# Attention's output added in halves from two buffers, its last block by single chunks, ending six tiles from the end

## The chip, the cores and the metric

One Trainium2 chip, one of its cores. The time is device microseconds of one execution. A profiled execution gives, besides its time, the span from the first to the last recorded instruction, in which all positions below are told. The engines are TensorE (PE, with its weight loads PEld), VectorE (DVE), ScalarE (ACT), GpSimd (POOL) and SyncE (SP), which only issues DMAs.

## What is computed

The input x is 8 sequences of 1024 tokens with 256 numbers each, in float32. It is normalised by token, and the output is the sum of three things: x itself, a causal linear attention over each sequence (16 heads of 16, kernel elu + 1), and a mixture of 8 experts of which each token takes 2.

```python
xn = _layernorm(x)
# attention
q = jax.nn.elu(q) + 1.0
k = jax.nn.elu(k) + 1.0
kv_cumsum = jnp.cumsum(jnp.einsum('blhd,blhe->blhde', k, v), axis=1)
out = jnp.einsum('blhd,blhde->blhe', q, kv_cumsum) / denom[..., None]
out.reshape(Bx, Lx, HIDDEN) @ Wo.T
# experts: c holds two weights a token
h = jax.nn.silu(gate) * up
out = jnp.einsum('bse,besh->bsh', c, jnp.einsum('besi,eih->besh', h, W2))
x = x + attention(xn) + experts(xn)
```

## The kernel before

**Attention** goes by blocks of 512 tokens (NBLK = 16, two to a sequence), each of four chunks of 128. `block_steps` (L1033) cuts a block into 9 steps: four project q, k and v and spread the denominators (`rden`, eight DMAs on SP's queue), one computes the first chunk's scores and closes the block before, four weigh the chunks. With one step after the last block there are LAST = 145 steps. `attend` (L1009) ends a chunk: two matmuls with Wo into `a_ps` (L1016), and ScalarE copies the result into a quarter of the tile `at` (L1021). `at` is a tile of four chunks, from a pool with one buffer. After the fourth chunk GpSimd issues one DMA of 512 KB that adds `at` to the rows of the output (L1027); of the last block three chunks go first (384 KB) and the fourth by itself (128 KB, L1025). A chunk is closed one step after it is weighed, the fourth in the fifth step of the next block.

**The experts** (FFN) go by tiles of 128 rows sorted by expert: NM = 132 tiles, 25 of the first four blocks and then 107. For tile j, `ffn_step` (L1345) issues the gathers of rows (`xg`) and of their weights and moments (`entry`) some tiles ahead on GpSimd's queue (L1217, L1222), the two 512 KB weight matrices of tile j + 2 on SP's queue (L1288, five buffers), and between them the DMA transpose of the normalised rows (L1249). TensorE makes `gu_ps` from them (L1307), ScalarE and VectorE make hT = silu(gate) * up (L1315, L1318), TensorE makes `y_ps` of the tile before (L1326), VectorE multiplies it by the routing weight into `y` (L1333, five buffers), and GpSimd adds those rows to the output by an indirect DMA (L1337, `ffn_store`). For the first 25 tiles and the first attention blocks the sums go to an accumulator in memory, `acc_d`, which is copied to the output after tile 26 (L1440); all others go to the output `out_dram`.

**Order.** The loop over tiles (L1389) calls `attend_upto(n)` ahead of each tile's `ffn_step`: it makes attention steps until n are made, at most one a tile except at the steps that may go together. From tile READ = 22 on, n rises in a straight line from 23 to 144 at tile 130, and the rest falls to tile 131 (L1433). Apart from the first stage, a scheduler places the instructions on the engines in an order near that of the program, and it inserts the waits. Every DMA that adds to `out_dram` waits until the one before it that touched `out_dram` has landed, whatever rows it writes; and an instruction that waits on GpSimd's queue holds back all that stand behind it there: stores, gathers, entries. The last tile is cut in two on TensorE, with the y matmuls of tile 130 between its two halves (`last`, L1296).

Of the kernel before, what the change touches and what calls it, by code (L numbers as in the profile page):

```python
# [46 lines left out]
F32 = mybir.dt.float32  # L47
# [4 lines left out]
ALU = mybir.AluOpType  # L52
AX = mybir.AxisListType

P = 128
# [9 lines left out]
def tile_attention_moe(  # L65
# [14 lines left out]
    nc = tc.nc  # L80
    B, L, H = x.shape
# [4 lines left out]
    NCH = TB // P  # L86
    N = B * L
    NBLK = N // TB
# [10 lines left out]
    NM = NF - NR  # L99
# [11 lines left out]
    one = ctx.enter_context(tc.tile_pool(name="one", bufs=1))  # L111
# [31 lines left out]
    for t in range(FB):  # L143
        xbs[t] = e_one.tile([P, NCH, H], F32, name=f"xb{t}")
        step = NCH // 2 if t == 0 else NCH
        for c in range(0, NCH, step):
            some = slice(c, c + step)
            in_order(nc.sync.dma_start(out=xbs[t][:, some, :], in_=xf[t][:, some, :]))

    def load_x(t, queue):  # L150
        xbs[t] = f_x.tile([P, NCH, H], F32, tag="xb", name=f"xb{t}")
        in_order(queue.dma_start(out=xbs[t], in_=xf[t]))
# [15 lines left out]
    for t in range(FB, FB + 2):  # L168
# [8 lines left out]
        out=causal, in_=causal, pattern=[[1, P]], compare_op=ALU.is_ge,  # L177
# [5 lines left out]
        out=before, in_=before, pattern=[[1, P]], compare_op=ALU.is_ge,  # L183
# [8 lines left out]
        out=own, in_=own, pattern=[[-HD, HALF]], compare_op=ALU.is_ge,  # L192
# [3 lines left out]
        out=own, in_=own, pattern=[[HD, HALF]], compare_op=ALU.is_ge,  # L196
# [105 lines left out]
    def moments(t, n):  # L302


        def small(name, *shape, dtype=F32):
            return f_two.tile([P, n * NCH, *shape], dtype, tag=name, name=name)

        less, rstd = (tab[:, t * NCH : (t + n) * NCH, w] for w in (1, 2))
        st = small("st", 6)
        mv = small("mv", 2)  # L310
        for c in range(n * NCH):
            nc.vector.bn_stats(st[:, c, :], xbs[t + c // NCH][:, c % NCH, :])
            nc.vector.bn_aggr(mv[:, c, :], st[:, c, :])
        v = small("v")
        nc.vector.tensor_scalar(v, mv[:, :, 1], EPS_NORM, None, ALU.add)
        half = small("half")
        nc.vector.tensor_scalar(half, v, -0.5, None, ALU.mult)
        bits = small("bits", dtype=I32)
        nc.vector.tensor_scalar(bits, v.bitcast(I32), 1, None, ALU.arith_shift_right)
        nc.vector.tensor_scalar(bits, bits, -1.0, float(0x5F3759DF), ALU.mult, ALU.add)  # L320
        y = bits.bitcast(F32)
        for i in range(4):
            sq = small("sq")
            nc.vector.tensor_tensor(sq, y, y, ALU.mult)
            nc.vector.tensor_tensor(sq, sq, half, ALU.mult)
            y_new = small(f"y{i % 2}") if i < 3 else rstd
            nc.vector.scalar_tensor_tensor(y_new, sq, 1.5, y, ALU.add, ALU.mult)
            y = y_new
        yield
        nc.vector.scalar_tensor_tensor(less, mv[:, :, 0], -1.0, rstd, ALU.mult, ALU.mult)  # L330
        yield

    def normalise(t):
        xb = xbs.pop(t)
        less, rstd = (tab[:, t * NCH : (t + 1) * NCH, w] for w in (1, 2))
        for c in range(NCH):
            if t < FB and (c % 2 == 0 or t == FB - 1):
                nc.vector.tensor_scalar(
                    xb[:, c, :], xb[:, c, :], rstd[:, c : c + 1], less[:, c : c + 1],
                    ALU.mult, ALU.add,  # L340
                )
            else:
                nc.scalar.activation(
                    xb[:, c, :], xb[:, c, :], AF.Identity, bias=less[:, c : c + 1],
                    scale=rstd[:, c : c + 1],
                )
        scaled[t] = xb
# [47 lines left out]
    def logits_turned(t):  # L395
        lgT = f_two.tile([P, P], F32, tag="lgT", name="lgT")
        nc.scalar.copy(lgT, logits(t))
        tp = ps_y.tile([P, P], F32, tag="y", name="lg_t")
        nc.tensor.transpose(tp, lgT, ident)
        return tp  # L400
# [398 lines left out]
    blocks = {}  # L799
# [207 lines left out]
    ats = {}  # L1007

    def attend(t, c, oT):  # L1009


        if c == 0:
            ats[t] = one.tile([P, NCH, H], F32, tag="at", name=f"at{t}")
        a_ps = ps_y.tile([P, H], F32, tag="y", name="a_ps")
        for hh in range(2):
            nc.tensor.matmul(  # L1016
                a_ps, lhsT=oT[:, hh, :], rhs=wo_sb[:, hh, :],
                start=(hh == 0), stop=(hh == 1),
            )
        at = ats[t]  # L1020
        nc.scalar.copy(at[:, c, :], a_ps)  # L1021
        to = acc_f if t < FB and not copied else of
        if t == NBLK - 1 and c >= NCH - 2:
            some = slice(0 if c == NCH - 2 else c, c + 1)
            nc.gpsimd.dma_start(out=to[t][:, some, :], in_=at[:, some, :], accum_op=ALU.add)  # L1025
        elif c == NCH - 1:
            nc.gpsimd.dma_start(out=to[t], in_=at, accum_op=ALU.add)  # L1027
        if c == NCH - 1:
            del ats[t], blocks[t]

    behind = []

# [28 lines left out]
    LAST = NBLK * STEPS + 1  # L1061
# [11 lines left out]
    def attend_upto(n, apart=True):  # L1073
        first = True
        while steps_made[0] < min(n, LAST):
            if apart and not first and steps_made[0] % STEPS not in TOGETHER:
                break
            next(steps)
            steps_made[0] += 1
            first = False  # L1080
# [90 lines left out]
    for a in range(4):  # L1171
        some = slice(a * E // 4, (a + 1) * E // 4)
        in_order(
            nc.sync.dma_start(
                out=w2_sb.rearrange("p (c h) -> p c h", h=H)[
                    :, a * E * IC // 4 : (a + 1) * E * IC // 4, :
                ],
                in_=w2[some].rearrange("e (c p) h -> p (e c) h", p=P),
# [7 lines left out]
    def copy_rows(a, b):  # L1186
# [6 lines left out]
        out=tab_d[0].rearrange("(p j i) w -> p j (i w)", j=2, i=FT),  # L1193
        in_=tab.rearrange("p (j i) w -> p j (i w)", j=2)[:, :, 0 : FT * 3],
# [33 lines left out]
    def ffn_norm(j):  # L1228
        in_order(
            nc.scalar.activation(  # L1230
                xg[j], xg[j], AF.Identity, bias=entry[j][:, 1:2], scale=entry[j][:, 2:3]
            )
        )
# [3 lines left out]
    def ffn_halves(j):  # L1237

        halves[j] = ffn2.tile([P, 2, H], U16, tag="half", name="half")
        nc.vector.tensor_copy(  # L1240
            halves[j], xg.pop(j).bitcast(U16).rearrange("p (h b) -> p b h", b=2)
        )
# [143 lines left out]
    LISTS = NBLK - FB  # L1386
    READ = LISTS + 10
    AHEAD = 2 + LISTS // 2 + 3 * (READ - LISTS) // 2
    for j in range(NM + 1):  # L1389
        if j + 1 < TURNED:  # L1390
            ffn_norm(j + 1)
        if TURNED <= j + 2 < NM:
            ffn_norm(j + 2)
            ffn_halves(j + 2)
        t = FB + j
        counting = FB < t <= NBLK and t % ROUND == 0
        if counting and t == NBLK:
            for _ in routing:
                pass
        if 0 < j and t < NBLK:  # L1400
            if j % 2 == 0:
                with tc.issue_after((last_token if j < 4 else last_masked)[0].ins):
                    for _ in moments(t, 2):
                        pass
            normalise(t)
            turn(t)
            if t + 5 < NBLK:
                load_x(t + 5, nc.scalar)
            add_logits(t, 1, logits_turned(t))
            if (t + 1) % ROUND == 0:  # L1410
                routing = route(t + 1 - ROUND, t + 1)
                next(routing)
        if j == LISTS:
            in_order(
                nc.sync.dma_start(
                    out=tab_d[1][1 : 1 + NS * P, :].rearrange("(p i) w -> p (i w)", p=P),
                    in_=tab.rearrange("p i w -> p (i w)"),
                )
            )
            in_order(nc.sync.dma_start(out=tab_d[1][0:1, :], in_=before[0:1, 0:3]))  # L1420
            lists = second_batch(taken)
        if LISTS <= j < READ:
            next(lists)
        if LISTS <= j < LISTS + NBLK - FB:
            t = FB + j - LISTS
            rows = slice(t * TB, (t + 1) * TB)
            in_order(nc.sync.dma_start(out=out_rows[rows, :], in_=x_rows[rows, :]))
        if j < LISTS:
            attend_upto(3 + j // 2)
        elif j < READ:  # L1430
            attend_upto(AHEAD - 3 * (READ - j - 1) // 2)
        else:
            attend_upto(AHEAD + (LAST - 1 - AHEAD) * (j - READ + 1) // (NM - 1 - READ) + j // (NM - 1))  # L1433
        ffn_step(j, LATE if N1 < j <= N1 + LATE else 0)
        if counting and j < LISTS:
            for _ in routing:
                pass
        if j == N1 + 1:
            copied.append(j)
            in_order(nc.sync.dma_start(out=out_rows[0 : FT * P, :], in_=acc_d[:, :]))  # L1440
# [54 lines left out]
```

## Time and profile before

| what | us |
|---|---|
| three timed runs, median (lowest to highest) | 1266.21 (1262.2 to 1268.4) |
| the profiled execution | 1262.54 |
| its span | 1260.7 |
| TensorE busy | 1217.8 (97%) |
| GpSimd busy | 522.2 (41%) |
| ScalarE waiting for the DMA of `at` before its copy L1021 | 27.7, in 6 places |

In the profile's lines a group is named by line, engine and operation, with what it writes and reads (`out_dram<-at` is the DMA that adds attention's output, `out_dram<-y,dst_i` a store of a tile's rows). The page's second part cuts the span into 40 slices with a digit for the busy tenths of each; its fourth part follows the work that ended last back to its releasers. A timeline line gives the start, the duration, the engine, and in brackets how long the engine had been idle before and what ended that. DMAs issued by GpSimd run on after their instruction has ended, so the instruction's own duration (1.6 us for a store) is not the transfer's.

Of the page's list of DMA issues, these bear on the change: `out_dram<-at` thirteen times with 512 KB, once with 384 KB and once with 128 KB; `acc_d<-at` twice with 512 KB; `out_dram<-y,dst_i` 107 times; `w<-in_w_dram` 264 times with 512 KB.

### The profile page before, as it was taken

The page shows a single profiled execution, that of the slowest core. Times are in us where ns is not written, and L with a number is a line of the kernel's source. Part 1 is how long each engine was busy: PE and PEld are TensorE (multiplying, and loading weights), DVE is VectorE, ACT ScalarE, POOL GpSimd, SP SyncE. Part 2 cuts the span into 40 slices and gives each one's busy share as a digit, 9 for nine tenths or more (in the row PEclk, how much of TensorE's full clock was granted, in tenths as well). Part 3 has the DMA queues.
Part 4 walks back from the last instruction along what each step waited for, and adds up shares of the span by engine and source line. Part 5 has one row for each costly group of instructions (what it writes and reads, how often), then busy time and mean ns, then how long its engine had stood idle before and what let it go on. Part 6 is the DMA issues. An engine that isn't in the chain of part 4 may idle for free.

```text
span 1260.7 us, 29753 instructions
## 1 busy us (share of the span) xinstructions
PE 1217.8 (97%) x11460; PEld 1058.2 (84%) x11460; DVE 674.5 (54%) x1541; ACT 560.9 (44%) x1068; POOL 522.2 (41%) x460
## 2 busy tenths in 40 slices
PE   7799999999999999999999999999999999999994
PEld 5578887787898989988888989989888889899884
DVE  7677589864354554545453545545453545445451
ACT  5666475461534526262624426262626344252620
POOL 4734233233334544443535444444443444443422
PEclk9899999999999999999999999999999999999998
DMA  9798565557788796979799797879896877969782
GB/s 334 278 288 255 174 192 118 181 157 224 212 191 196 173 235 155 228 176 219 161 196 207 164 224 155 219 180 207 184 215 161 197 193 168 218 157 231 166 177 35
DMA packets 203934, 245.84 MB, mean 195 GB/s; under 512 B 72946, under 2 KB 127858, under 8 KB 203506
## 3 DMA queue, kind: packets, MB, share of 16 engines
q1 hardware_dynamic: 161010, 191.79, 52.5%
q0 software_dynamic: 38032, 43.22, 24.2%
q10 hardware_dynamic: 4752, 8.91, 2.1%
q8 instruction: 94, 1.54, 0.5%
q14 instruction: 46, 0.38, 0.1%
HBM read 187.91 MB, written 44.29 MB: 184 GB/s over the span
## 4 chain that ended last, share of the span: by engine, by line
PE 87%; DVE 5%; ACT 3%; DMA 3%; issue 1%; POOL 0%; SPq 0%; POOLq 0%; DVEq 0%; ACTq 0%
PE gu_ps L1307 37%; PE y_ps L1326 17%; PE s_ps L937 5%; PE o_ps L974 5%; PE a_ps L1016 5%; PE zq L820 4%; PE zkv L836 4%; PE zkk L836 4%; PE o_ps L956 2%; DMA xb<-in_x_dram 1%; PE tp L358 1%; DMA out_dram<-y,dst_i 1%; PE tp L883 1%; PE lg_ps L378 1%; DMA out_dram<-at 1%
## 5 line engine op out<-in xcount | busy, mean ns | idle before, releaser
L1307 PE MATMUL gu_ps<-xgT,w 128*128 128x128 f32 x4224 | 509.3, 277 | 0.5 <-ACT xgT L1270 0.5
L1307 PEld LDWEIGHTS gu_ps<-xgT,w 128*128 128x128 f32 x4224 | 489.1, 192 | 20.0 <-issue 14.4
L1337 POOL DMA_INDIRECT out_dram<-y,dst_i x107 | 175.2, 1638 | 328.3 <-DVE s_sb L944 103.3
L1326 PE MATMUL y_ps<-w_sb,hT 128*128 x1056 | 251.0, 380 | 1.8 <-DVE hT L1318 1.6
L1217 POOL DMA_INDIRECT xg<-in_x_dram,src_i x132 | 129.1, 978 | 240.1 <-DVE half L1240 109.9
L1326 PEld LDWEIGHTS y_ps<-w_sb,hT 128*128 128x128 f32 x1056 | 190.4, 191 | 23.6 <-DVE hT L1318 2.0
L944 DVE TENSOR_TENSOR s_sb<-s_ps,causal 128x512 f32<-128x512 f32 x256 | 159.8, 682 | 81.5 <-PE s_ps L937 75.2
L1315 ACT ACTIVATE hT<-gu_ps 128x512 f32<-128x512 f32 x132 | 78.8, 597 | 277.1 <-PE gu_ps L1307 207.5
L1222 POOL DMA_INDIRECT entry<-tab_d,of_i x107 | 106.4, 995 | 42.3 <-issue 31.4
L1318 DVE TENSOR_TENSOR hT<-gu_ps,hT 128x512 f32<-128x512 f32 x132 | 90.3, 684 | 61.9 <-PE gu_ps L1307 33.0
L1240 DVE COPY half<-xg 128x512 uint16<-128x512 uint16 x105 | 47.5, 453 | 134.9 <-ACT xg L1230 134.9
L1333 DVE TENSOR_SCALAR y<-y_ps,entry 128x256 f32<-128x256 f32 x132 | 63.6, 482 | 99.8 <-PE y_ps L1326 99.5
L1021 ACT COPY at<-a_ps 128x256 f32<-128x256 f32 x64 | 23.8, 372 | 172.1 <-PE a_ps L1016 123.7
L937 PE MATMUL s_ps<-qm,kT 32*128 32x256 f32 x1024 | 85.4, 404 | 0.5 <-DVE hT L1318 0.4
L1258 ACT COPY xgT<-halfT 128x512 uint16<-128x512 uint16 x105 | 79.7, 759 | 6.5 <-DMA halfT<-half 6.5
L1230 ACT ACTIVATE xg<-xg,entry 128x256 f32<-128x256 f32 x132 | 78.6, 596 | 4.1 <-DMA entry<-tab_d,num_i 3.4
L1016 PE MATMUL a_ps<-wo_sb,oT 128*128 128x256 f32 x256 | 68.2, 387 | 3.0 <-DVE oT L991 2.7
L974 PE MATMUL o_ps<-s_sb,va 128*32 128x128 f32 x2048 | 69.9, 276 | 0.0
L974 PEld LDWEIGHTS o_ps<-s_sb,va 128*32 128x32 f32 x2048 | 52.3, 109 | 17.9 <-issue 15.3
L937 PEld LDWEIGHTS s_ps<-qm,kT 32*128 32x128 f32 x1024 | 50.6, 184 | 18.6 <-issue 9.3
L1337 POOL DMA_INDIRECT acc_d<-y,src_i x25 | 40.9, 1637 | 53.0 <-DVE y L1333 15.1
L836 PE MATMUL zkv<-wkv_sb,xnT 128*128 128x256 f32 x256 | 59.6, 386 | 0.0
(228 smaller groups left out, 1353.9 us busy)
## 6 DMA issues: line engine op xcount, KB each, us to landing
w<-in_w_dram SPq DMA_DIRECT2D x264, 512.0 KB
rden<-over SPq DMA_DIRECT2D x128, 64.0 KB
xnT<-xnT_d SPq DMA_DIRECT2D x15, 512.0 KB
out_dram<-at POOLq DMA_DIRECT2D x13, 512.0 KB
out_dram<-in_x_dram SPq DMA_DIRECT2D x12, 512.0 KB
xnT_d<-xnT ACTq DMA_DIRECT2D x11, 512.0 KB
xb<-in_x_dram SPq DMA_DIRECT2D x9, 512.0 KB
w_sb<-in_w_dram SPq DMA_DIRECT2D x4, 1024.0 KB
```

The costliest lines, as they stand in the source:

```text
L836: nc.tensor.matmul(z[:, i, :], lhsT=xnTs[t][:, k, bass.ts(c + i, P)], rhs=wkv_sb[:, k, a, :], start=(k == 0), stop=(k == KC - 1),)
L937: nc.tensor.matmul(s_ps[r][:, hh].rearrange("p a l -> p (a l)"), lhsT=kT[rows, hh, span], rhs=qm[rows, hh, :, span], start=True, stop=True,)
L944: last_masked[0] = nc.vector.tensor_tensor(sm, s_ps[r].rearrange("p k a l -> p (k a) l"), causal_b, ALU.mult)
L974: nc.tensor.matmul(o_ps[32 * r : 32 * r + 32, hh, :], lhsT=va[:, c, 4 * hh + r, a, :], rhs=s_sb[r][:, 2 * hh + a, :], start=(first and a = ...
L1016: nc.tensor.matmul(a_ps, lhsT=oT[:, hh, :], rhs=wo_sb[:, hh, :], start=(hh == 0), stop=(hh == 1),)
L1217: rows = nc.gpsimd.indirect_dma_start(out=xg[j], out_offset=None, in_=x_rows[:, :], in_offset=bass.IndirectOffsetOnAxis(ap=src_i[:, i : i ...
L1222: nc.gpsimd.indirect_dma_start(out=entry[j], out_offset=None, in_=table[:, :], in_offset=bass.IndirectOffsetOnAxis(ap=num_i[:, i : i + 1], ...
L1258: nc.scalar.copy(xgT[j].bitcast(U16).rearrange("p k (l b) -> p b k l", b=2), halves.pop(j).rearrange("p (b k) l -> p b k l", b=2),)
L1307: done = nc.tensor.matmul(ps[:, i, :], lhsT=w13[:, k, bass.ts(i, P)], rhs=xgT[j][:, k, :], start=(k == 0), stop=(k == KC - 1),)
L1318: nc.vector.tensor_tensor(hT, gu[1], hT, ALU.mult)
L1326: done = nc.tensor.matmul(y_ps, lhsT=hT[:, i, :], rhs=w2_sb[:, bass.ds(e * (IC * H) + i * H, H)], start=(i == 0), stop=(i == IC - 1),)
L1337: nc.gpsimd.indirect_dma_start(out=rows[:, :], out_offset=bass.IndirectOffsetOnAxis(ap=dst_i[:, i : i + 1], axis=0), in_=ys.pop(j), in_off ...
```

## The change

`at` becomes two tiles of two chunks, `at0` and `at1`, each with a buffer of its own. After every second chunk the two are added by a DMA of 256 KB. Of the last block each chunk is added by itself (128 KB). The count of attention steps is taken from a new function, `spread(j)`: a straight line from tile 22 to 140 steps at tile 116 (SLOW = NM - 16), then one step in every two tiles, so that the last of 145 is made ahead of tile 125's `ffn_step`.

```diff
-        if c == 0:
-            ats[t] = one.tile([P, NCH, H], F32, tag="at", name=f"at{t}")
+        half = c // 2
+        if c % 2 == 0:
+            ats[t, half] = one.tile([P, NCH // 2, H], F32, tag=f"at{half}", name=f"at{half}")
...
-        at = ats[t]
-        nc.scalar.copy(at[:, c, :], a_ps)
+        at = ats[t, half]
+        nc.scalar.copy(at[:, c % 2, :], a_ps)
         to = acc_f if t < FB and not copied else of
-        if t == NBLK - 1 and c >= NCH - 2:
-            some = slice(0 if c == NCH - 2 else c, c + 1)
-            nc.gpsimd.dma_start(out=to[t][:, some, :], in_=at[:, some, :], accum_op=ALU.add)
-        elif c == NCH - 1:
-            nc.gpsimd.dma_start(out=to[t], in_=at, accum_op=ALU.add)
+        alone = t == NBLK - 1
+        if alone or c % 2:
+            some = slice(c, c + 1) if alone else slice(c - 1, c + 1)
+            nc.gpsimd.dma_start(
+                out=to[t][:, some, :], in_=at[:, some.start % 2 : c % 2 + 1, :],
+                accum_op=ALU.add,
+            )
...
+    SLOW = NM - 16
+
+    def spread(j):
+        most = LAST - 5
+        if j <= SLOW:
+            return AHEAD + (most - AHEAD) * (j - READ + 1) // (SLOW - READ + 1)
+        return min(LAST, most + (j - SLOW + 1) // 2)
+
...
-            attend_upto(AHEAD + (LAST - 1 - AHEAD) * (j - READ + 1) // (NM - 1 - READ) + j // (NM - 1))
+            attend_upto(spread(j))
```

More of the change, by code (lines that the diff above doesn't have):

```diff
@@ L1019, in attend @@
             )
-        at = ats[t]
-        nc.scalar.copy(at[:, c, :], a_ps)
+        at = ats[t, half]
+        nc.scalar.copy(at[:, c % 2, :], a_ps)
         to = acc_f if t < FB and not copied else of
-        if t == NBLK - 1 and c >= NCH - 2:
-            some = slice(0 if c == NCH - 2 else c, c + 1)
-            nc.gpsimd.dma_start(out=to[t][:, some, :], in_=at[:, some, :], accum_op=ALU.add)
-        elif c == NCH - 1:
-            nc.gpsimd.dma_start(out=to[t], in_=at, accum_op=ALU.add)
+        alone = t == NBLK - 1
[5 more added lines that the diff above has]
+            )
+        if c % 2:
+            del ats[t, half]
         if c == NCH - 1:
-            del ats[t], blocks[t]
+            del blocks[t]
     behind = []
```

## Prediction

> **What bounds the kernel now.** I read the slices of the span first, then busy time by stretch, then the chain that ended last, and then GpSimd's timeline, because the chain ends there.
>
> ```profile
> span 1260.7 us, 29753 instructions
> PE 1217.8 (97%) x11460; PEld 1058.2 (84%) x11460; DVE 674.5 (54%) x1541; ACT 560.9 (44%) x1068; POOL 522.2 (41%) x460
> ...
> PE   7799999999999999999999999999999999999994
> ```
>
> TensorE is idle at the two ends only. The stretches say it in figures (after the window: its length, then busy us of PE, PEld, DVE, ACT, POOL, the granted clock, the DMA share and GB/s):
>
> ```profile
> 400.00:1000.00 600.00, 600.00 (x5624) 532.70 (x5623) 290.14 (x534) 262.91 (x441) 271.52 (x224) 1.00 0.85 191
> 1000.00:1229.00 229.00, 229.00 (x2291) 203.04 (x2290) 113.72 (x211) 92.69 (x157) 90.71 (x74) 1.00 0.83 191
> 1229.00:1246.00 17.00, 15.80 (x131) 14.10 (x129) 5.14 (x11) 2.45 (x5) 5.48 (x4) 1.00 0.32 41
> 1246.00:1261.00 15.00, 0.00 (x0) 0.00 (x0) 0.17 (x1) 0.00 (x0) 3.15 (x2) 0.66 0.24 26
> ```
>
> From 400 to 1229 us TensorE has no idle time at a granted clock of 1.00; a wait removed from another engine there shortens nothing. The last 15 us hold no matmul at all. The chain that ended last shows what they hold (start us, us, what):
>
> ```profile
> 1234.06 5.74 DMA out_dram<-at
> ...
> 1240.55 3.95 DMA out_dram<-y,dst_i
> ...
> 1245.05 3.03 DMA out_dram<-at
> ...
> 1248.83 3.90 DMA out_dram<-y,dst_i
> ...
> 1253.78 1.25 POOL out_dram L1337
> ```
>
> Every addition to the output, a tile's rows (y) or attention's block (at), waits until the one before has landed. The last y matmul begins at 1243.66 and lasts 1.99, so TensorE ends at **T = 1245.65**, and 15.05 us follow. Two attention pieces of 384 and 128 KB stand among the last stores. GpSimd's timeline says where the queue came from:
>
> ```profile
> 1201.28 1.58 POOL L1337 DMA_INDIRECT out_dram<-y,dst_i  x1 [6.50 <-DVE y L1333]
> 1207.06 1.39 POOL L1027 DMA_DIRECT2D out_dram<-at  x1 [4.20 <-DMA out_dram<-y,dst_i]
> 1219.86 1.66 POOL L1337 DMA_INDIRECT out_dram<-y,dst_i  x1 [11.40 <-DVE s_sb L944]
> ```
>
> Block 14's 512 KB held the chain from 1207.06 to 1219.86, 12.8 us.
>
> **The change, part by part.**
>
> *Halves.* Blocks 0 to 14 make 30 pieces of 256 KB instead of 15 of 512 KB, and the last block four of 128 KB instead of two: 34 issues for 17. GpSimd spends 1.39 us on a 512 KB issue and 0.91 us on the last, 128 KB one, so 17 more cost it at most 24 us of 1260, in idle time (41% busy). Each piece waits on ACT's copy and on the landing before it; the gather and the stores behind it on GpSimd wait too. A gather is issued three to four tiles before its rows are normalised, some 30 us, and y has five buffers, so a piece of 5 to 7 us reaches nobody. If it did, ScalarE's normalisation and then TensorE would wait for rows.
>
> *Two buffers.* ScalarE's copy L1021 waits 27.7 us in 6 places for "DMA out_dram<-at". That goes. In those stretches TensorE is already busy all the time: worth nothing, bounded by 0 and 27.7, and I take 0 because TensorE shows no idle time to give back.
>
> *Denser attention.* Up to tile 116 attention makes 117 steps in 95 tiles (1.23 a tile) instead of 121 in 109 (1.11); then one step in two tiles; the last after tile 125's start. The matmuls are the same in number, and in the built order of the changed kernel a step still stands between gu and y groups. Changes between full and 32-wide matmuls cost about 0.1 us each and shift by a handful either way: 0, within 1 us. So TensorE's end stays at T if it is fed.
>
> *The end.* After store 121 can be issued, TensorE still has, by the chain's rows: the step with chunk 2 (a_ps 0.86, o_ps 0.54, 0.90, 0.24: 2.5), two FFN tiles (gu 3.57 and y 1.73: 5.30 each, 10.6), chunk 3's 0.86, six FFN tiles alone (31.8), and the halved last tile (1237.34 to 1245.65: 8.3). That is 54.0 us. With 0.48 for the multiplication by the weight and 0.3 to the issue, store 121 may go at T-53.2 and store 131 at T+0.85. In between the chain must carry ten stores (121 to 130) and two 128 KB pieces. From issue to next issue a quiet store takes **4.65** (1248.83 to 1253.48) and a quiet 128 KB piece **3.78** (1245.05 to 1248.83). After the last issue 7.2 us follow (1253.48 to 1260.70).
>
> - All quiet: the chain keeps up until the last three stores, which come at only 3.6 and 4.6 us spacing (T-7.5, T-3.8, T+0.85). Store 129 at T-7.5 plus two of 4.65 gives T+1.8 for store 131, the end T+9.0, against T+15.05: **6.0 us gained**.
> - Loaded: weights run until about T-12. GpSimd's timeline has stores that wait for each other under load:
>
> ```profile
> 1158.83 1.62 POOL L1337 DMA_INDIRECT out_dram<-y,dst_i  x1 [3.06 <-DVE s_sb L944]
> ...
> 1163.45 1.63 POOL L1337 DMA_INDIRECT out_dram<-y,dst_i  x1 [0.45 <-issue]
> ...
> 1168.09 1.62 POOL L1337 DMA_INDIRECT out_dram<-y,dst_i  x1 [0.46 <-DVE y L1333]
> ```
>
> 4.62 and 4.64, with an entry and a gather between them. Others take longer: 1201.28 to 1207.06 (5.78), 1117.75 to 1124.17 (6.42, behind a gather). So a loaded store is bounded by 4.62 and 6.42. I take **5.0**, nearer the quiet end, as no block of 512 KB and no spreading of denominators (rden) falls in this stretch, while weights come faster than before. A loaded 128 KB piece lies between 3.78 and half of the slowed 512 KB one (6.4); I take 4.2, near the row of its own size. Seven loaded stores (121 to 127), three quiet ones and two pieces: 35.0 + 13.95 + 8.4 = 57.35. Store 131 goes at T+4.15, the end is T+11.4 = 1257.05: **3.6 us gained**.
>
> One rule speaks against the change. The Trainium skill, "DMA: Bandwidth & Descriptors", section on the anatomy of one DMA on the GpSimd path, gives each DMA a fixed cost near 2 us plus its bytes at 436 GB/s, so that cutting transfers up multiplies the fixed part. The rows agree in kind: 128 KB took 3.03 us and 384 KB 5.74, a straight line that leaves 1.7 us at no bytes. By the page four pieces of 128 KB would take 9.2 us where 384 and 128 KB took 5.2, by the rows 12.1 where 8.8; both make the chain's work longer, and only where it lies can make it cheaper. By the page's 2.3 us a piece in place of 4.2 the sum would gain 6.0.
>
> **Sum.** The span falls from 1260.7 to 1257.1, the profiled execution from 1262.54 to 1258.9. The three timed runs have the median 1266.21, 3.7 above the profiled one; I take the same 3.6 off it: **1262.6**.
>
> **Rivals.**
>
> - *The chain stays quiet* (4.65 throughout): 6.0 gained, **1260.2**. For it: 4.62 and 4.64 above at a DMA share of about 0.7. Against it: FFN tiles alone ask for more. Chance 0.22.
> - *The chain is the bound and overflows.* Pairs of tiles with one step bring two stores and a piece in about 14.2 us (two tiles 10.6, a step 3.6). From 117 on the chain carries eleven loaded stores, three quiet and four pieces in 81.6 us; it ends as late as before at 5.3 us a store with 4.4 a piece (58.3 + 13.95 + 17.6 - 81.6 + 7.2 = 15.4 after T). At 5.8 and 4.5, the queue late enough that two more stores go quiet, nine loaded: 52.2 + 23.25 + 18.0 - 81.6 + 7.2 = 19.1 after T, 4 us **slower**, about **1270.3**; at 6.4 some 10 us. It decides from 5.3 us. For it: 5.78 and 6.42; against it: those had a gather or rden alongside. Chance 0.15.
> - *The weights come late.* An FFN tile alone needs 1.05 MB of weights, and 0.13 each of gather, store, its read and the transpose: 1.57 MB in 5.3 us is 296 GB/s. The stretches show 335 in the first 32 us, 299 at 1150, but 263 to 268 at 1206 to 1214. At 268 a tile takes 5.9 us, 0.6 more on six tiles: 3.6 us later, less what lies loaded ahead (two and a half tiles of buffers). I price it at 2.5, which leaves a gain of about 1: **1265**. Chance 0.12.
> - *The likeliest*, 3.6 gained: chance 0.51.
>
> **Numbers.** Predicted 1262.6. 0.5% is 6.3 us, about what a measurement of this kernel can tell from no change (its runs lie 6.2 us apart). The quiet case stands on that edge: 0.09 of its 0.22 lies beyond it, and 0.07 of the likeliest: faster 0.16. The overflowing chain passes 6.3 in the larger part of its chance, 0.09, with 0.01 from late weights: slower 0.10. Same 0.74. The range takes in the quiet case less 2 us of spread and the overflowing chain at 5.8: 1258 to 1270.5.
>
> **What would show it.** Right: TensorE without idle time from 400 us to its last matmul, its end within 1 us of 1245.65, the copies' wait for the DMA of at gone, no at among the last eight additions, 9 to 13 us after the last matmul. The quiet case shows GpSimd waiting for y (DVE) before the last stores but two; the overflow shows each of the last ten stores waiting for the one before, 5.5 us and more apart. Late weights would show TensorE idle before gu (a DMA of w as the releaser) in the last 40 us. I am wrong altogether if the middle changes: if rows arrive late behind the more numerous pieces, if the copy of the accumulator to the output at 337 us is held up by a piece that now goes to the accumulator, or if the denser attention stalls TensorE.

## The result and the profile after

The changed kernel takes 1274.23 us (median of 20 runs, 1266.43 to 1277.9) where the kernel before took 1264.95 beside it (20 runs, 1261.54 to 1274.27): a ratio of 1.0062, 95% interval 1.0049 to 1.0076. It is slower by 0.6%, where 3.6 us of gain were forecast. The profiled execution took 1275.46 us with a span of 1273.8, 13.1 more than the span before. That is more than the 9.3 us between the medians: the profiled execution of the kernel before lies 2.4 us under its median, that of the changed kernel 1.2 over its own.

The page and the stretches of the changed kernel, in the columns known from before:

```profile
span 1273.8 us, 29815 instructions
PE 1221.6 (96%) x11460; PEld 1063.4 (83%) x11460; DVE 674.6 (53%) x1541; ACT 560.0 (44%) x1068; POOL 545.9 (43%) x477
...
PE   7899999999999999999999999999999999999991
```

```profile
400.00:1229.00 829.00, 828.58 (x7943) 737.98 (x7942) 404.59 (x749) 352.99 (x597) 375.77 (x309) 1.00 0.86 190
1229.00:1246.00 17.00, 16.15 (x115) 15.02 (x113) 4.50 (x8) 3.10 (x5) 4.74 (x3) 1.00 0.53 104
1246.00:1274.00 28.00, 0.24 (x2) 0.00 (x0) 0.48 (x1) 0.00 (x0) 7.78 (x5) 0.55 0.22 24
```

TensorE is as full as before: 0.42 us idle in the 829 us from 400 to 1229, and its last matmul ends at 1246.24 (1245.65 before). Nearly all of the 13.1 us lies behind that: 27.5 us from the last matmul to the end, where there were 15.05. The last stretch holds five GpSimd instructions, and they are stores. GpSimd's timeline from the first late store on (start, duration, instruction, in brackets its idle time before and what ended it; gathers and entries between them are left out, here and in the timelines below):

```profile
1167.86 1.63 POOL L1342 DMA_INDIRECT out_dram<-y,dst_i  x1 [3.38 <-DVE s_sb L944]
...
1173.59 0.97 POOL L1027 DMA_DIRECT2D out_dram<-at  x1 [2.81 <-DMA out_dram<-y,dst_i]
...
1178.65 1.62 POOL L1342 DMA_INDIRECT out_dram<-y,dst_i  x1 [2.74 <-DVE y L1338]
...
1190.03 1.06 POOL L1027 DMA_DIRECT2D out_dram<-at  x1 [3.81 <-ACT hT L1320]
...
1196.69 1.62 POOL L1342 DMA_INDIRECT out_dram<-y,dst_i  x1 [4.25 <-DMA out_dram<-at]
...
1209.73 0.96 POOL L1027 DMA_DIRECT2D out_dram<-at  x1 [2.46 <-ACT xgT L1263]
...
1217.06 1.63 POOL L1342 DMA_INDIRECT out_dram<-y,dst_i  x1 [5.02 <-DMA out_dram<-at]
...
1227.28 0.97 POOL L1027 DMA_DIRECT2D out_dram<-at  x1 [1.59 <-issue]
1233.78 1.63 POOL L1342 DMA_INDIRECT out_dram<-y,dst_i  x1 [5.53 <-DVE y L1338]
1238.38 1.56 POOL L1342 DMA_INDIRECT out_dram<-y,dst_i  x1 [2.97 <-issue]
...
1261.83 1.56 POOL L1342 DMA_INDIRECT out_dram<-y,dst_i  x1 [2.96 <-issue]
1266.37 1.56 POOL L1342 DMA_INDIRECT out_dram<-y,dst_i  x1 [2.98 <-DMA out_dram<-y,dst_i]
```

The four single pieces of the last block are the lines with `at`. Their periods, from the piece's start to the next addition's, are 5.06, 6.66, 7.33 and 6.50: 6.39 in the mean. The seven stores from 1167.86 on (117 to 123) take 5.77 in the mean. The last weights are issued at 1230.47, and from 1236 to 1240 the DMA traffic has fallen to 34 GB/s. The seven stores 124 to 130, from 1233.78 on, take 4.66 in the mean (4.48 to 4.60, one of them 5.42): the same instruction, quiet. The last issue at 1266.37 leaves 7.43 to the end.

The clearest view is how late each store starts after VectorE has made its y (worked out from the two engines' timelines, us):

| store | 117 | 118 | 119 | 120 | 121 | 122 | 123 | 124 | 125 | 126 | 127 | 129 | 131 |
|---|---|---|---|---|---|---|---|---|---|---|---|---|---|
| before | 0.3 | 12.2 | 11.7 | 7.3 | 0.3 | 0.3 | 1.1 | 1.7 | 0.3 | 11.4 | 8.0 | 3.4 | 7.3 |
| after | 3.7 | 5.4 | 4.8 | 9.2 | 11.5 | 16.4 | 16.8 | 21.7 | 21.0 | 17.3 | 17.4 | 18.6 | 19.2 |

Before, a block of 512 KB throws the chain back by some 12 us, and three tiles later it is on time again. After, the pieces are smaller and the chain is never on time again. The reason is the distance between the tiles: y of tile 115 and y of tile 131 are 129.6 us apart before (8.1 a tile) and 96.4 after (6.03), because the attention steps that lay between those tiles have been made earlier. A store of 5.77 in a tile of 6.03 leaves 0.26 us for everything else.

The wait that the change was aimed at is gone. ScalarE's copies before and after, from the list of its waits (in total, times, longest):

```profile
ACT at L1021 <- DMA out_dram<-at: 27.7, 6, 5.5
```

```profile
ACT at L1022 <- PE a_ps L1017: 137.4, 52, 6.0
```

No line of the changed kernel has a copy wait for the DMA. No gain shows for it; TensorE had not been waiting for it.

### The profile page after: what moved, and what is told of

Same layout as the page of the kernel before. It is cut to its first block, busy times and chain, and to the rows that moved or that the text cites. A ratio compares the mean times of both kernels' runs of the same rounds, so it can differ in the third digit from the quotient of the medians.

```text
span 1273.8 us, 29815 instructions
## 1 busy us (share of the span) xinstructions
PE 1221.6 (96%) x11460; PEld 1063.4 (83%) x11460; DVE 674.6 (53%) x1541; ACT 560.0 (44%) x1068; POOL 545.9 (43%) x477
## 5 line engine op out<-in xcount | busy, mean ns | idle before, releaser
L1027 POOL DMA_DIRECT2D out_dram<-at x29 | 37.1, 1280 | 81.6 <-DMA out_dram<-y,dst_i 39.9
L974 PEld LDWEIGHTS o_ps<-s_sb,va 128*32 128x32 f32 x2048 | 52.8, 110 | 18.1 <-issue 15.5
```

The lines of the kernel that those rows point to most:

```text
L974: nc.tensor.matmul(o_ps[32 * r : 32 * r + 32, hh, :], lhsT=va[:, c, 4 * hh + r, a, :], rhs=s_sb[r][:, 2 * hh + a, :], start=(first and a = ...
```

## The experiments

The overflow of the chain was a rival in the prediction. What had to be told apart was why its transfers were so long, and which part of the change fills the chain. The first theory, L, is the load: weights for fast tiles take the DMA engines while the additions run. Its rival, Q, is GpSimd's own queue, the gathers and entries between the stores. The runs lay on four chips. On one the kernel before took 1265.16 us, on the others 1286.22, 1286.04 and 1285.09. So each ratio is against the kernel before on the same chip, and tails (from the last matmul's end to the end of the span) are compared within one chip first.

### Half of the change at a time

The halves and the single pieces, with the pace of before:

```diff
-            attend_upto(spread(j))
+            attend_upto(AHEAD + (LAST - 1 - AHEAD) * (j - READ + 1) // (NM - 1 - READ) + j // (NM - 1))
```

> The halves and two buffers, with the last block by single chunks, at the old pace (last attention step at tile 131). Theory L (load): an addition to the output takes 5.8 us for a store and 6.4 us for a 128 KB piece only while tiles without attention pull weights in fast; at the old pace of 8.3 us a tile the chain of additions keeps up, and 12 to 17 us follow TensorE's last matmul: 1262 to 1267 us, within 0.3% of the kernel before. Theory N (number): seventeen more additions make the chain too long wherever they stand: over 20 us after the last matmul, 1269 us or more.

Measured: 1286.28 us, ratio 0.998 (0.9951 to 1.0008), a tail of 16.2, as theory L has it.

The pace alone, with the kernel before's one tile `at`, blocks of 512 KB and the last block as 384 and 128 KB:

```diff
-            attend_upto(AHEAD + (LAST - 1 - AHEAD) * (j - READ + 1) // (NM - 1 - READ) + j // (NM - 1))
+            attend_upto(spread(j))
```

> The new pace alone (117 steps up to tile 116, then one in two tiles, the last at tile 125), with whole blocks of 512 KB in one buffer and the last block in 384 and 128 KB. Theory L: the pace makes the loss by itself: 20 us or more after the last matmul, 1269 to 1277 us. Theory N: with only two pieces among the last sixteen stores instead of four the chain fits: 9 to 14 us after the last matmul, 1259 to 1264 us.

Measured: 1289.08 us, ratio 1.0009 (0.9981 to 1.0037), a tail of 26.0. GpSimd's timeline of this run has the long tail with no single piece in it but the last:

```profile
1221.42 1.41 POOL L1025 DMA_DIRECT2D out_dram<-at  x1 [4.56 <-DMA out_dram<-y,dst_i]
1229.10 1.64 POOL L1337 DMA_INDIRECT out_dram<-y,dst_i  x1 [4.90 <-DVE y L1333]
1236.41 1.62 POOL L1337 DMA_INDIRECT out_dram<-y,dst_i  x1 [3.12 <-DMA out_dram<-y,dst_i]
1243.35 0.97 POOL L1025 DMA_DIRECT2D out_dram<-at  x1 [4.03 <-issue]
```

The store between the two pieces takes 7.31 us (1229.10 to 1236.41), the next 6.94. Store 121 is 4.5 us late, store 124 is 19.8. So the pace makes the tail; the halves and pieces alone do not. In time the two runs can't be told from the kernel before, nor clearly from each other, although theory L expected a loss of 4 us or more from the pace. On this chip TensorE's end itself differed between the four profiled executions by up to 6 us (1261.6 to 1267.7): the pace's tail is 9.8 us longer than that of the halves, but its TensorE ends 4.6 us earlier. So these two runs show the tail alone; a pair of runs on one chip, further down, shows the pace's cost in time.

### The load taken away

The changed kernel without the loads of weights from tile 116 on (the matmuls use tile 115's, so the last tiles' results differ):

```diff
+        if SAME <= j < NM:
+            if halved:
+                ffn_turn_halves(j)
+            for s in range(2):
+                ws[j, s] = kept_w[s]
+            return
```

> The changed kernel, which from tile 116 on loads no weights and uses those of tile 115 again (the last sixteen tiles' part of the output is left wrong by that). Theory L: stores fall to 4.6 to 4.9 us and pieces to 3.8 to 4.2 us from issue to issue, store 131 goes out 2 to 5 us after the last matmul, 9 to 12 us follow it: 1255 to 1259 us. Theory N or a theory Q, that the rows and entries gathered on the same GpSimd queue hold the stores up: periods stay at 5.8 and 6.4 us and 25 us or more follow: 1270 us or more.

Measured: 1279.25 us, ratio 0.994 (0.9907 to 0.9972), a tail of 10.7. The stretch 1160 to 1240 of the changed kernel, in the profile of the result, and of this one (the last two columns are the DMA share and GB/s):

```profile
1160.00:1240.00 80.00, 80.00 (x712) 75.53 (x711) 26.37 (x52) 23.05 (x42) 35.21 (x29) 1.00 0.96 216
```

```profile
1160.00:1240.00 80.00, 79.82 (x763) 73.84 (x762) 31.65 (x61) 22.05 (x42) 41.83 (x35) 1.00 0.49 72
```

And its timeline, with the gathers of rows left where they were:

```profile
1218.85 0.96 POOL L1027 DMA_DIRECT2D out_dram<-at  x1 [1.41 <-ACT hT L1331]
1223.78 1.63 POOL L1353 DMA_INDIRECT out_dram<-y,dst_i  x1 [2.23 <-DMA out_dram<-at]
1228.42 1.62 POOL L1353 DMA_INDIRECT out_dram<-y,dst_i  x1 [0.47 <-issue]
1232.76 0.97 POOL L1027 DMA_DIRECT2D out_dram<-at  x1 [1.45 <-ACT xg L1235]
1236.88 1.63 POOL L1353 DMA_INDIRECT out_dram<-y,dst_i  x1 [3.15 <-DMA out_dram<-at]
```

Stores of 4.64 and 4.34, pieces of 4.93 and 4.12, and no store of the last 15 more than 3.3 us late. The changed kernel itself was not run on this chip, but the pace alone was, with its weights and a spacing of 6.01: its stores 117 to 123 took 6.3 to 7.5. The spacing here (6.04 a tile) and the gathers are those of the changed kernel, so the load of weights is what lengthens the additions. Q is not needed. Taking the gathers away instead was not tried.

The Trainium skill, "DMA: Bandwidth & Descriptors", section on queues, rings and completion order, says that a DMA engine goes round the queues that have work for it and empties one packet of each at a time. Pieces of 128 KB that take 4.1 to 4.9 us without the weights' queue beside them and 5.1 to 7.3 with it agree with that; no run here shows single packets.

### The last block's pieces taken out of the chain

The changed kernel, with the last block's four pieces written to memory of their own by another queue (they are not added to the output):

```diff
+            if alone:
+                nc.scalar.dma_start(out=apart_d[c], in_=at[:, c % 2, :])
+            else:
...
```

> The changed kernel, with the last block's four pieces written to memory of their own by ACT's queue, so that they leave the chain of additions (the last block's attention is missing in the output). Four pieces of 6.4 us are 26 us of chain: with stores of 5.8 us under load the fourteen stores from 117 on need 73 us of the 82 there are, so the chain keeps up and 9 to 12 us follow the last matmul: 1256 to 1261 us, if load and pieces together make the overflow. If stores alone are too slow for tiles of 5.3 us, so that the pieces hardly matter: 18 us or more after the last matmul, 1266 us or more.

Measured: 1284.35 us, ratio 0.9971 (0.9942 to 1.0001), a tail of 14.6, of which 10.3 lie after the last store's issue (7.43 in the changed kernel). It is neither the 9 to 12 of one expectation nor the 18 of the other; without those 2.8 us more at the very end it would be the first. Under full load (DMA share 0.96 from 1160 to 1240) the stores alone nearly keep up with the fast tiles: at most 4.9 us late over the last fifteen, although three of them (122 to 124) took 7.0 to 7.2 each. So the overflow is loaded stores and the last block's pieces together: the stores use up the tiles, the pieces have no room.

### On one chip: the pieces' size and the place of the end

> The changed kernel once more, on the chip of this call, so that its tail is read beside the others' there. Theory L (the last tiles' weight loads make each accumulating transfer longer, 5.8 us a store and 6.4 us a 128 KB piece, so that the chain falls some 20 us behind TensorE's end): 26 to 28 us from the last matmul's end to the span's end, and a ratio of 1.004 to 1.008. If the lengthening belonged to one chip or one execution: 12 to 17 us after the last matmul and a ratio of 0.997 to 1.000.

Measured: 1277.15 us, ratio 1.008 (1.0053 to 1.0108), a tail of 26.7. The long tail is no accident of one execution.

> The kernel before once more, on the chip of this call. Under theory L its tail depends on the work queued after the loads end (its last block's pieces come when no weights are loaded) and stays near 15 us. If its tail is as long as the changed kernel's here, what differs between chips is the tail of both, and the ratio says nothing about the pace.

Measured: 1264.23 us, ratio 0.9988 (0.9969 to 1.0007), a tail of 13.6. So 13.1 us of tail part the two kernels here, and 12.9 us of median time: the tail is most of the loss. In these two profiles TensorE's end differs as well, by 4.0 us (1248.7 against 1244.7); where they come from is told in the part on the prediction.

The changed kernel with the last block in two halves:

```diff
-        alone = t == NBLK - 1
+        alone = False
```

> The changed kernel, but the last block goes out in two halves of 256 KB instead of four pieces of 128 KB; the pace is the changed kernel's. Theory L with a price for each transfer (6.4 us a piece whatever it holds, near 9 for a half): 4 x 6.4 - 2 x 9 = 7.6 us less of the chain, a tail of 18 to 22 us and a ratio of 1.000 to 1.004. If the price goes by bytes alone (12.8 us a half under load): the tail stays at 26 to 28 us and the ratio with the changed kernel's.

Measured: 1271.22 us, ratio 1.0044 (1.0026 to 1.0062), a tail of 25.0. The two halves took 10.74 us (behind it a gather) and 7.32:

```profile
1184.40 1.33 POOL L1027 DMA_DIRECT2D out_dram<-at  x1 [1.49 <-ACT xgT L1263]
1195.14 1.63 POOL L1342 DMA_INDIRECT out_dram<-y,dst_i  x1 [8.04 <-DVE oT L991]
...
1222.25 1.32 POOL L1027 DMA_DIRECT2D out_dram<-at  x1 [3.61 <-DMA out_dram<-y,dst_i]
1229.57 1.64 POOL L1342 DMA_INDIRECT out_dram<-y,dst_i  x1 [6.00 <-issue]
```

18.1 us, where four single pieces took 25.6 to 26.3: the price falls with the number of transfers, as expected, but little of it reaches the end (1.7 us of tail; the medians differ by 5.9, and their intervals overlap). The expectation of 18 to 22 failed: the stores between took 6.1 to 8.1 instead.

Halves for every block, the last too, at one straight pace that ends two tiles before the last:

```diff
-        alone = t == NBLK - 1
+        alone = False
...
+    DONE = NM - 1 - 2
...
-            attend_upto(spread(j))
+            attend_upto(AHEAD + (LAST - AHEAD) * (j - READ + 1) // (DONE - READ + 1))
```

> Halves for every block, the last too, at one straight pace that ends two tiles before the last. Theory L: no more transfers than two 256 KB halves in the last tiles where the changed kernel has four single pieces and a half, and the second of them starts when the loads have ended; a tail of 9 to 14 us, a ratio of 0.994 to 0.999. Rival (the halves themselves are what costs, wherever they are put): a tail of 20 us or more, a ratio of 1.003 or more.

Measured: **1259.76 us, ratio 0.9957 (0.994 to 0.9973)**, a tail of 12.1. On this chip this beats both kernels. It differs from the run above in the pace alone, and is 11.5 us faster with 12.9 us less tail: so the pace costs time, and not only tail. Its tiles are 8.06 us apart, as before, and its timeline at the end is this:

```profile
1207.83 1.55 POOL L1342 DMA_INDIRECT out_dram<-y,dst_i  x1 [5.88 <-DVE y L1338]
1216.56 1.54 POOL L1342 DMA_INDIRECT out_dram<-y,dst_i  x1 [7.18 <-DVE y L1338]
1220.84 1.27 POOL L1027 DMA_DIRECT2D out_dram<-at  x1 [2.74 <-issue]
1227.70 1.64 POOL L1342 DMA_INDIRECT out_dram<-y,dst_i  x1 [5.59 <-DVE oT L991]
1232.13 1.26 POOL L1027 DMA_DIRECT2D out_dram<-at  x1 [2.80 <-DMA out_dram<-y,dst_i]
1237.23 1.64 POOL L1342 DMA_INDIRECT out_dram<-y,dst_i  x1 [3.84 <-DMA out_dram<-at]
```

The two stores in front of the last block's halves wait for their y (DVE): the chain is on time there. The last half takes 5.10, and four stores follow it. Its tail is 1.5 to 3.0 us shorter than in the two profiles of the kernel before; the medians differ by 5.4. Where the rest is, these profiles do not show: TensorE ends no earlier (1246.9 against 1245.7 and 1244.7), and the profiled executions of the kernel before (1262.54 and 1260.09) were faster than its medians, so that they hardly differ from the one here (1260.68).

### Where the end lies, and which part costs what

The changed kernel with its single pieces and its end six tiles early, but a straight pace up to there:

```diff
+    DONE = NM - 1 - 6
...
-            attend_upto(spread(j))
+            attend_upto(AHEAD + (LAST - AHEAD) * (j - READ + 1) // (DONE - READ + 1))
```

> The changed kernel with its halves, its four single pieces and its end six tiles ahead of the last, but the attention steps at one straight pace up to there, with no tile in two left without a step. Theory S (the spacing of the stores: tiles that hold no step follow each other in 5.3 us where tiles with one take 8 or more, and the changed kernel strews eight such tiles over its last sixteen while the weights load, so that a chain of 5.8 us a store and 6.4 us a piece falls behind from there): only the last six or seven tiles are short, the chain comes into them at most 5 us late, a tail of 10 to 17 us, a ratio of 0.994 to 1.001. Rival (four single pieces, or an end six tiles early, is what costs): a tail of 22 us or more, a ratio of 1.003 or more.

Measured: 1289.49 us, ratio 1.0021 (0.9994 to 1.0048), a tail of 22.2. Theory S by itself falls: this is the rival's tail, with the spacing mended except in the last tiles. The ratio decides nothing.

Halves instead of single pieces, ending six, four and one tile before the last (the number in DONE):

> As the run with halves at a straight pace that ended two tiles from the end, but ending six from the end. Theory S: six short tiles at 5.3 us against 4.6 to 5.8 a store leave the chain 0 to 4 us late, a tail of 9 to 15 us, a ratio of 0.993 to 0.999. If ending early costs by itself: worse than the run that ends two tiles from the end by more than 5 us of tail.

Measured: 1285.16 us, ratio 0.9978 (0.9949 to 1.0006), a tail of 17.8, where 9 to 15 were expected.

> The same, ending four tiles from the end. Theory S: the last half is away about 25 us ahead of TensorE's end, the stores behind it are some 3 us late at most; a tail of 9 to 13 us, a ratio of 0.993 to 0.998.

Measured: 1287.92 us, ratio 0.9997 (0.9967 to 1.0028), a tail of 17.5, where 9 to 13 were expected.

> The same, ending one tile from the end. Theory S: the last half of 256 KB (5 us when nothing loads) is issued within 10 us of TensorE's end, among the last quiet stores, which leaves 2 to 4 of them behind it; a tail of 12 to 17 us, a ratio of 0.995 to 1.000, no better than the runs that end two to four tiles early.

Measured: 1285.64 us, ratio 0.9997 (0.9967 to 1.0027), a tail of 15.0, within what was expected, though shorter than with four tiles, where no better was expected. The ratios of these three can't be told apart. Beside the 12.1 of the run that ended two tiles early, on another chip, the tails suggest that ending earlier than that costs, although the last tiles then carry stores alone. To settle the parts on one chip, a ladder from the changed kernel undid them one by one:

> The changed kernel, as the end of a ladder on one chip. If its three parts (taper over the last sixteen tiles, single pieces, end six tiles early) each cost something: a tail of 25 to 29 us here and shorter tails on every step of the ladder.

> The taper undone, the single pieces and the end six tiles early kept. By the run on the other chip 22 us of tail, 4 to 6 less than the changed kernel. If theory S holds alone: 10 to 17.

> The single pieces undone as well, the end six tiles early kept. By the run on the other chip 18 us of tail, 4 less than with single pieces. If pieces go by bytes alone, the same tail as with single pieces.

> The end put back to two tiles ahead of the last. If an early end costs by itself, since the last tiles then follow each other in 5.3 us while weights load: 11 to 14 us of tail, 4 to 7 less than six tiles early, and a ratio of 0.993 to 0.998. If the difference seen so far was that between two chips: the same tail as with six, and no ratio below 0.998.

| run | us | ratio (95%) | tail | lateness of stores 121, 123, 125, 127, 131 |
|---|---|---|---|---|
| the changed kernel | 1294.41 | 1.0061 (1.0028 to 1.0095) | 21.8 | 6.2, 11.2, 15.2, 13.7, 13.8 |
| without the taper | 1291.82 | 1.0055 (1.0034 to 1.0076) | 20.6 | 2.3, 5.1, 12.1, 12.0, 12.6 |
| and without single pieces | 1287.9 | 1.0019 (0.9993 to 1.0044) | 17.9 | 1.8, 3.3, 10.3, 8.9, 10.1 |
| and ending two tiles early | 1282.52 | 0.9987 (0.9968 to 1.0006) | 12.1 | 2.9, 2.1, 0.3, 2.3, 4.4 |

The steps of the tail are 1.2, 2.7 and 5.8 us; the medians fall by 2.6, 3.9 and 5.4. Each tail is that of one profiled execution, and two profiles of one kernel differed by 0.8 and 1.4 us above, so the first step, the taper, is not shown to cost anything: the intervals of its two ratios overlap almost wholly. The single pieces and the end six tiles early cost, by the tails the end the most; for the pieces the two runs six tiles from the end on the chip before say the same (22.2 against 17.8 of tail, 4.3 us between the medians). Three expectations missed here: the changed kernel's tail is shorter on this chip (21.8, not 25 to 29), undoing the taper took 1.2 us off it instead of 4 to 6, and the last run's ratio (0.9987) lies just above the 0.993 to 0.998 given, so that on this chip it can't be told from the kernel before. In the lateness, the third row shows what an early end does: the chain is nearly on time at store 123 and falls back 7 us over the next two, in tiles that follow each other in 5.3 us while their weights load. The block's last half falls into the same stretch and takes 7.4 us, where it takes 5.4 in the last row.

## Why the prediction was wrong

- **TensorE and the middle: right in the first profile, not in the second.** In the first its end moved by 0.6 us (within 1 was given), and it idled 0.42 us from 400 to 1229. In the second profile of the changed kernel it ends at 1248.7, 4.0 us later than the kernel before on that chip, with two gaps of 2.0 and 1.6 us in front of y matmuls that wait for VectorE's hT, none for weights: late weights were not the case. The lines below the list show where these gaps come from.
- **Two buffers: right.** 27.7 us of ScalarE's wait went, and no run shows a gain from it.
- **Halves: right.** With the pace of before (first experiment) they can't be told from the kernel before. But that a piece "reaches nobody" holds only while the chain is on time.
- **"Store 121 may go at T-53.2": the readiness was right.** VectorE made its y at T-53.4 (1192.83). But the store started at T-41.9 (1204.37), 11.5 us later: the likeliest case began its count at 121 with an empty chain, and the chain was not empty.
- **"A loaded 128 KB piece ... I take 4.2, near the row of its own size" and "a loaded store ... I take 5.0": the steps that failed.** From store 117 the chain was to carry, in the rival's own count, 11 loaded stores, 3 quiet and 4 pieces. With 5.0 and 4.2 that gives 55.0 + 13.95 + 16.8 - 81.6 + 7.2 = 11.4 after T, the forecast again, so a longer count alone would not have saved it. Measured from store 117's start at T-78.4: 7 x 5.77 + 4 x 6.39 + 7 x 4.66 - 78.4 + 7.4 = 27.6, where the trace has 27.5. Of the 16.1 us between the two, the pieces are 4 x (6.39 - 4.2) = 8.8, the seven loaded stores 7 x 0.77 = 5.4, the late start 3.2; the four stores that went out quiet, since they were so late, give back 1.4. The piece was priced by a row of its own size taken after the loads had ended. Its other bound, half of the slowed 512 KB block (6.4), is what was measured, but by luck: such a half is 256 KB, and the two halves of 256 KB took 10.74 and 7.32. The stores' rows of 4.62 and 4.64 stood at a DMA share of 0.68 to 0.76, where the changed kernel has 0.96 from 1160 to 1240; and the second is no price at all, since the store at 1168.09 went out 0.3 us after its y and waited for VectorE, not for the chain.
- **The rival "the chain is the bound and overflows" is what happened**, at a chance of 0.15, and it was priced at 1270.3 with 19.1 us after T. Its store of 5.8 was exact (5.77); its piece of 4.5 was short by 1.9 four times, 7.6 of the 8.4 us that were missing. "No at among the last eight additions" came true and meant nothing: eight stores were queued instead. "The last ten stores 5.5 us and more apart" was wrong: the queue was carried past the end of the loads and ran off at 4.5 to 5.4.
- **The rule of the page.** By the anatomy section of "DMA: Bandwidth & Descriptors" in the Trainium skill a 128 KB transfer is an estimated 2.3 us. Measured: 3.0 to land with nothing beside it, periods of 5.1 to 7.3 with weights beside it. What follows from a fixed cost, that cutting up multiplies it, agrees with the last block's 512 KB: 25.6 to 26.3 us as four pieces, 18.1 as two halves. The page's figure does not agree.
- **The range** (1258 to 1270.5) missed the time by 3.7 us, because the overflow was taken in with a piece at 4.5. With the upper bounds that the text itself names, 6.42 and 6.4, the range would have reached past it.

How the late chain reached TensorE is read from the second profile of the changed kernel:

```profile
1219.57 1.63 POOL L1342 DMA_INDIRECT out_dram<-y,dst_i  x1 [4.24 <-DMA out_dram<-at]
1221.50 0.98 POOL L1227 DMA_INDIRECT entry<-tab_d,of_i  x1 [0.30 <-issue]
```

```profile
1224.37 0.60 ACT L1235 ACTIVATE xg<-xg,entry 128x256 f32<-128x256 f32 x1 [6.07 <-DMA entry<-tab_d,of_i]
```

```profile
1226.08 1.99 PE L1331 MATMUL y_ps<-w_sb,hT 128*128 x8 [1.98 <-DVE hT L1323]
```

Store 122 waits for a single piece to land and goes out 20.6 us late; the gather of a tile's weights and moments (`entry`) stands behind it on GpSimd's queue; ScalarE waits 6.07 us for that before it can normalise the rows; VectorE makes hT behind its copy of these rows (1225.00 and 1225.35), and TensorE waits for hT. It is the way that the prediction names under "Halves" and takes for closed. In the first profile ScalarE waits there too (3.56 and 2.66 us), and TensorE does not.

What stays open: why the tail of the changed kernel is 5 us shorter on one chip than on another (there the four pieces took 4.4 to 6.5 us, some 4 less in all, and store 117 went out 2.2 earlier; the profiled execution was 4.5 us faster than the median); and how much of the four-tile and six-tile ends' tails belongs to the chips they ran on beyond the ladder.

## What to carry to other kernels

A chain that carries one transfer at a time pays back a delay only by the difference between the spacing of its jobs and the price of one job: 8.1 against 4.6 to 5.8 a tile repaid a 12 us block in three tiles, 6.03 against 5.77 repaid nothing. Work on the bottleneck engine that is moved out of a stretch shortens that stretch, and with it packs its loads and its stores closer, so count what else must fit there. Price a transfer by rows under the load that it will run in, whatever their size, and when one price stands several times in a sum, carry both its ends through the sum before choosing the range.

## What the runs showed of the hardware

- In the changed kernel one and the same store takes 4.5 to 4.6 us from issue to issue (once 5.4) with no weights loading and 5.8 in the mean (4.5 to 7.7) with them; a 128 KB addition takes 3.8 quiet, 4.1 to 4.9 beside gathers and stores alone, 6.4 (5.1 to 7.3) beside weights at a DMA share near 1, and 4.4 to 6.5 on another chip. The load lengthens them in the mean, not each of them: in the run with the last block apart a store took 4.56 (from 1237.63) at a DMA share of 1.00 and 265 GB/s.
- The last issue's landing took 10.3 us instead of 7.2 to 7.6 in the one run in which ScalarE's queue had written pieces to memory; no run tells why.
- Four chips ran the same kernel before in 1265 us (one) and 1285 to 1286 (three). In the runs on the slower ones TensorE is idle for 33 to 42 us between its first and its last matmul, against 23 to 31 in the others, and its last matmul ends at 1262 to 1272 instead of 1245 to 1249.
- After the last matmul the granted clock falls to 0.5, 2.5 us later in the changed kernel (from 1248.8 on) and 5.1 us later in the kernel before (from 1250.8 on). The mean clock of 0.982 against 0.991 is mostly that longer tail (25.0 us at half clock to the end of the span where there were 10.0), not a slower TensorE: the stretches from 400 to 1246 show 1.00.
